# Third set's moments and second set's scaling by VectorE inside the second layer's attentions, with another order of stages there and in the last mixture

## The chip, the cores and the metric

The kernel runs on one core of one Trainium2 chip. The metric is the device time of one execution in microseconds (us). Six runs of the kernel before took 1302.55, 1298.72, 1302.09, 1302.53, 1300.03 and 1296.94 us; their median is 1301.06 us.

## The reference

The reference is a pre-LN decoder of two layers over `x`, 32 batches of 128 positions of 128 features, with a context `ctx_1024` of the same shape. Everything is float32. Cut to what matters:

```python
x = x + attn0(layernorm(x))              # 16 heads of 8, rotated, softmax
x = x + xattn0(layernorm(x), ctx)        # 16 heads of 64, relu between two output weights
x = x + moe0(layernorm(x))               # 16 experts, 4 per token, chosen by groups, and a shared one
x = x + attn1(layernorm(x))              # random features: exp(phi), no softmax
x = x + xattn1(layernorm(x), ctx)        # 16 heads of 8, softmax
h = layernorm(x)                         # (x - mean) / sqrt(var + 1e-5)
logits = h @ gate_w.T
sel = top_k(logits + expert_bias, 4)     # 4 of 16 experts for each token
w = softmax(logits[sel])
routed = sum(w[e] * (silu(h @ w1[e].T) * (h @ w3[e].T)) @ w2[e].T for e in sel)
x = x + routed + (silu(h @ sw1.T) * (h @ sw3.T)) @ sw2.T
```

## The kernel before

**Tiling.** The 32 batches are 8 groups `x[g]` of 4 batches (`GB = 4`), one SBUF tile `[128 positions, 4, 128 features]` for each; two groups, 8 batches, are a set, so there are four sets, 0 to 3. Layer 0's attentions and its mixture take the first 785 us. Layer 1's two attentions (`second_layers`, some 785 to 1053 us) go group by group, four steps a group; the last mixture (`last_layer`, some 1052 to 1297 us) follows.

**The last mixture.** Sets 0, 2 and 3 (`SETS = (0, 2, 3)`; `n2`, `n3` are the latter two) are sent by expert: each token's normalised row is written by GpSimd's indirect DMA to the rows of its four experts in DRAM (`way_out`, L2236, 32 transfers a set), four tiles of 128 rows, a quad, are loaded by SyncE with the weights of their experts (`rows_of`, L2299, tiles `rows` and `row_weights`), turned (`rows_turned`, L2317, `prows`), multiplied (`rows_up`, `pg<-hrows` and `sgrows`; `rows_down`), and written back on ScalarE's queue (`rows_out`). GpSimd gathers each token's four rows again (`way_back`, L2349, `back`, 32 a set), and VectorE adds them to `x` with the token's four weights (`added`, L2360). There are 33 quads, one a step, from step 3 on. Set 1 (groups 2 and 3) is computed densely: every expert over every token (`chunk_up`, `chunk_down`), its `sg` scaled by a broadcast of the token's weight, the `share`, that SyncE fetches in blocks of 1 MB (`fetched`, L2276).

Before a set can be sent it is normalised, its logits are made (`routing`), experts chosen (`chosen`, in `route`), and places counted (`placed`, L2163 to L2217; the list of each tile's expert, `of`, comes at its end; `owned` transposes it on TensorE, `powner`, and makes it readable for the address registers). Sets 0 and 2 go through this inside the second attentions: `rnorm`, `rscaled`, `rturn`, `routing`, `choose`, `send` are stages of the last mixture that `second_layers` writes between the attention's own, six groups in all (0 and 1, 2 and 3, 4 and 5). Set 3, groups 6 and 7, is ready only when the attentions end, and is normalised in the last mixture.

**Two ways to normalise.** `moments` (L1138, L1139) makes mean and variance of a group on VectorE, two instructions a batch. The inverse root is made by GpSimd's `pow` (`power`, L1120) in `norm_factors`, or on VectorE by three Newton steps (`rsqrt`, L1109 to L1114; with the addition of epsilon at L1172, 12 small instructions a group) in `norm_factors_by_vector`. `normed` (L1149) then scales the four batches; batches 1 and 3 are done by the engine `second`, GpSimd unless named otherwise:

```python
for b in range(GB):
    eng = second if b % 2 else nc.vector
    eng.tensor_scalar(n[:, b, :], x[g][:, b, :], mv[:, b, 0:1], r[:, b : b + 1], ALU.subtract, ALU.mult)
```

In the last mixture's stages inside the attentions it was `second=nc.gpsimd`; the scaled rows of sets 1 and 2 are kept in the context tiles (`ctx` in the profile), those of set 0 in a tile of weights no longer used (`wide`). Set 3's are the tiles `xr`, scaled by VectorE alone.

**Order.** `steps` takes a list of stages, each with its first step, its distance in steps and its count, and writes them step by step. In each step, the stages of the first list advance in turn by one piece, and after each of them one piece of the stages in `between` is written, the first in that list that still has one. A stage with a fifth entry may not begin before the stages named there are written. From step `as_written` on (8 in `second_layers`, 0 in `last_layer`) the engines take the instructions in the order in which they were written: TensorE, VectorE, ScalarE, GpSimd, and in the last mixture SyncE too. So the order of the two lists is the order of the instructions of one step on every engine's queue, and a wait at the head of a queue holds everything behind it.

**Tile names of the second attentions.** In the first of them `xn`, `pxn` are the normalised group and its transposition, `pS` and `sb` the sums over keys (`totals`), `fsums`, `frec` the products with the queries (`average`), `proj` the output weights (`finish`). In the second, `pk`, `k`, `pval`, `vs`, `pq`, `qb` are its projections, `scores`, `e`, `sums` the softmax, `by_token`, `rec`, `a`, `aT` the division and transposition, `proj` the output.

Of the kernel before, what the change touches and what calls it, by code (L numbers as in the profile page):

```python
# [17 lines left out]
GB = 4  # L18
GT = GB * S
NG = T // GT  # L20
# [939 lines left out]
def fast_decoder(ctx: ExitStack, tc: tile.TileContext, ins, spans, out: bass.AP):  # L960
# [3 lines left out]
    nc = tc.nc  # L964
# [13 lines left out]
    last = [None]  # L978
# [164 lines left out]
    def normed(wk, g, mv, r, n=None, second=nc.gpsimd):  # L1143

        if n is None:
            n = wk.tile([128, GB, D], F32, name="xn", bufs=2)
# [3 lines that stand above are left out]
            if b % 2:  # L1150
                yield
        return n
# [728 lines left out]
        yield  # L1881
        return comb

    def mixture(tag, W, route, per, last, weights_of, more={}, kept=lambda g: None):


        nch = E // per
# [6 lines left out]
            xn[g] = yield from norm_factors(g)  # L1894

        def scaled(wk, g):
            xn[g] = yield from normed(wk, g, *xn[g], kept(g))

        def turn(wk, g):
            pool, bufs = (edge, 2) if g in groups(0) else (wk, 5)  # L1900
# [188 lines left out]
    class Tables:  # L2089


        def __init__(self, spare, C):

            self.C = C
            self.xn, self.ones, self.masks, self.parts, self.places, self.of, self.owners, self.placing = ({} for _ in range(8))
# [152 lines left out]
    def last_layer(tag, W, stages, of_expert, tables):  # L2248
# [7 lines left out]
        factors, held, ys, sgs, outs = ({} for _ in range(5))  # L2256
        of_set = lambda n: range(n * NBR // GB, (n + 1) * NBR // GB)

        def norm(g):
            factors[g] = yield from norm_factors_by_vector(g)  # L2260

        def scaled(g):
            xn[g] = wk.tile([128, GB, D], F32, name="xr", bufs=2)
            yield from normed(wk, g, *factors.pop(g), xn[g], nc.vector)

        def turn(g):
            hs[g] = wk.tile([128, GT], F32, name="hx", bufs=2)
# [193 lines left out]
        to_send = lambda n, many: [(n, [(u, k) for u in range(i, i + many) for k in range(4)]) for i in range(0, NBR, many)]  # L2461
        once = lambda stage, k, s: (lambda _: stage(k), s, 1, 1)
        steps(
            fetch_at(4, 3),
            fetch_at(7, 18),
            (each(rows_turned, quads), Q, 1, NQ),
            fetch_at(5, 9),
            fetch_at(6, 9),
            fetch_at(0, 0),
            fetch_at(1, 0),  # L2470
            fetch_at(2, 0),
            (several(each(rows_of, quads), (0, 1)), 0, 1, 1),
            fetch_at(3, 0),
            (ups, 0, 1, LAST),
            (each(rows_down, quads), Q + 1, 1, NQ),
            once(routing, n3, 7),
            once(tables.owned, n3, 15),
            (each(rows_up, quads), Q, 1, NQ),
            (several(turn, of_set(n3)), 5, 1, 1),
            (downs, 0, 1, LAST),  # L2480
            (lambda _: not_ok(wk), 29, 1, 1),
            (lambda _: chunk_up(*last), 50, 1, 1),
            (last_parts, 52, 1, GB + 1),
            once(tables.owned, n2, 3),
            between=[
                (each(added, batches(n3)), 39, 2, NBR),
                once(tables.placed, n2, 1),
                once(chosen, n3, 8),
                once(tables.placed, n3, 9),
                (each(way_back, batches(n3)), 38, 2, NBR),  # L2490
                (each(rows_of, quads[2:]), Q, 1, NQ - 2),
                (each(tables.way_out, to_send(n3, 1)), 10, 1, NBR),
                (each(added, batches(n2)), 30, 1, NBR),
                once(several(norm, of_set(n3)), None, 3),
                (each(tables.way_out, to_send(n2, 2)), 1, 1, 4),
                once(several(scaled, of_set(n3)), None, 5),
                (each(way_back, batches(n2)), 29, 1, NBR),
                (each(way_back, batches(0)), 17, 1, NBR),
                (each(added, batches(0)), 21, 1, NBR),
            ],  # L2500
            as_written=0,
            others=("SP",),
# [190 lines left out]
    def second_layers(stages, early, late, after, tables):  # L2693

        wk = phase("l1", attention_psum)
        late.append(wk)
        norm, scaled, turn_in, project, turn, features_q, features_k, totals, average, finish = stages
        xnorm, xscaled, xvalues, xkey, xturn, xproject, xweights, xaverage, xfinish = l1_xattn(early, wk)
        rnorm, rscaled, rturn, routing, choose, send, *_ = after
        R = NBR // GB  # L2700
        first = lambda stage: lambda g: stage(early, g)
        later = lambda stage: lambda g: stage(g + 1)
        norm_, scaled_ = later(norm), later(scaled)
        of_four = lambda stage, b, at: (lambda g: stage(g * GB + b), at, 4, NG)
        to_send = [(u, k) for u in range(NBR) for k in range(4)]

        steps(
            (finish, 9, 4, NG),
            (features_q, 3, 4, NG),
            (lambda _: tables.owned(0), 35, 1, 1),  # L2710
            (totals, 5, 1, NU),
            (later(turn), 6, 4, NG - 1),
            (xvalues, 11, 4, NG),
            (lambda _: send(early, 1), 43, 1, 1),
            (features_k, 4, 4, NG),
            (later(project), 5, 4, NG - 1),
            of_four(xweights, 1, 13),
            of_four(xweights, 2, 14),
            (xturn, 11, 4, NG, xscaled),
            (average, 5, 1, NU),  # L2720
            (xfinish, 17, 4, NG),
            (first(rturn), 20, 4, 3 * R),
            of_four(xweights, 3, 15),
            (later(turn_in), 4, 4, NG - 1),
            (xaverage, 13, 1, NU),
            (first(routing), (24, 33, 42), 1, 3),
            of_four(xweights, 0, 12),
            (xproject, 11, 4, NG),
            (xkey, 10, 4, NG),
            between=[  # L2730
                (lambda _: choose(2, 6), 43, 1, 3),
                (lambda k: tables.place(0, (7, -1)[k]), 32, 1, 2),
                (first(rscaled), 19, 4, 3 * R, xturn),
                (xscaled, 11, 4, NG),
                (lambda _: choose(1, 3), 35, 1, 6),
                (scaled_, 2, 4, NG - 1),
                (lambda _: choose(0, 3), 27, 1, 6),
                (first(rnorm), 18, 4, 3 * R),
                (xnorm, 9, 4, NG),
                (norm_, 0, 4, NG - 1),  # L2740
                (lambda i: tables.way_out(0, to_send[3 * i : 3 * i + 3]), 36, 1, 11),
            ],
            as_written=8,
        )
# [49 lines left out]
    with tc.tile_pool(name="l1early", bufs=1, reuse_waits="tile") as early:  # L2794
        late = []
        W1A, W1X, L = (load(name, nc.sync, early) for name in ("w1a", "w1x", "later"))
        with scope():
            stages = []

            def l1_setup(_, k):  # L2800
                stages.extend(l1_attn(early, late))

            mixture_layer(
                "l0f",
                mixture0,
                (l1_setup, *(lambda _, k, i=i: stages[i](k) for i in range(5))),
            )
# [46 lines left out]
```

## Time and profile before

| | |
|---|---|
| median of six runs | 1301.06 us (1296.94 to 1302.55) |
| the profiled execution's own time | 1298.54 us |
| its span | 1296.8 us, granted clock 0.982 on average |
| TensorE matmuls (PE) | 1205.9 us busy, 93% |
| weight loads (PEld) | 802.8 us, 62%, beside PE |
| VectorE (DVE) | 855.7 us, 66% |
| ScalarE (ACT) | 589.3 us, 45% |
| GpSimd (POOL) | 533.4 us, 41% |

The shares are averages over stages with different limits. The stretch that the change touches, from 980 us on, looks like this (PE and VectorE busy in 20 us each, from the windows):

| window, us | PE | DVE | POOL | granted clock |
|---|---|---|---|---|
| 980 to 1000 | 16.29 | 17.08 | 2.58 | 0.92 |
| 1000 to 1020 | 18.15 | 17.67 | 8.75 | 1.00 |
| 1020 to 1040 | 13.50 | 10.36 | 16.69 | 0.83 |
| 1040 to 1060 | 17.43 | 16.14 | 15.64 | 1.00 |
| 1060 to 1080 | 17.40 | 17.50 | 12.85 | 1.00 |
| 1080 to 1100 | 18.76 | 10.62 | 15.36 | 1.00 |

A row of a timeline gives start, duration, engine, line, operation, tile out<-in, shapes, a count, and in brackets the idle time before the row and what ended it.

### The profile page before, as it was taken

The page shows a single profiled execution, that of the slowest core. Times are in us where ns is not written, and L with a number is a line of the kernel's source. Part 1 is how long each engine was busy: PE and PEld are TensorE (multiplying, and loading weights), DVE is VectorE, ACT ScalarE, POOL GpSimd, SP SyncE. Part 2 cuts the span into 40 slices and gives each one's busy share as a digit, 9 for nine tenths or more (in the row PEclk, how much of TensorE's full clock was granted, in tenths as well). Part 3 has the DMA queues.
Part 4 walks back from the last instruction along what each step waited for, and adds up shares of the span by engine and source line. Part 5 has one row for each costly group of instructions (what it writes and reads, how often), then busy time and mean ns, then how long its engine had stood idle before and what let it go on. Part 6 is the DMA issues. An engine that isn't in the chain of part 4 may idle for free. (4 is left out here: it accounts for less than half of the span.)

```text
span 1296.8 us, 27100 instructions
## 1 busy us (share of the span) xinstructions
PE 1205.9 (93%) x10588; PEld 802.8 (62%) x10588; DVE 855.7 (66%) x2298; ACT 589.3 (45%) x884; POOL 533.4 (41%) x715
## 2 busy tenths in 40 slices
PE   7779999999999999988999998899998789999997
PEld 5447667777777778753444444666666446787754
DVE  5746767686868667566866554688888776524563
ACT  4545444545455543432332224466664544554532
POOL 6244242434342213413200012456542677477775
PEclk9889999999999999999999999999999899999998
DMA  9401132111111111244541602000000049899933
GB/s 326 143 2 34 34 109 64 35 35 34 35 35 34 35 34 35 72 96 113 113 100 33 132 1 104 1 3 2 2 2 3 24 157 307 288 318 286 287 94 102
DMA packets 82895, 118.62 MB, mean 91 GB/s; under 512 B 9032, under 2 KB 58056, under 8 KB 81352
## 3 DMA queue, kind: packets, MB, share of 16 engines
q1 hardware_dynamic: 70280, 92.95, 25.7%
q0 software_dynamic: 6144, 12.60, 3.3%
q10 hardware_dynamic: 6336, 11.26, 2.3%
q8 instruction: 86, 1.41, 0.5%
q14 instruction: 49, 0.40, 0.1%
HBM read 89.71 MB, written 27.07 MB: 90 GB/s over the span
## 5 line engine op out<-in xcount | busy, mean ns | idle before, releaser
L1311 ACT ACTIVATE e<-scores 128x1024 f32<-128x1024 f32 x128 | 124.0, 1021 | 79.3 <-PE scores L981 79.3
L981 PE MATMUL y<-sg,wide 128*128 128x512 f32 (+1 forms) x206 | 107.1, 611 | 5.3 <-DVE sg L2374 4.7
L2349 POOL DMA_INDIRECT back<-rows_out,place x96 | 92.8, 967 | 31.4 <-issue 24.7
L1149 POOL TENSOR_SCALAR xn<-x,mv,r 128x128 f32<-128x128 f32 x78 | 69.3, 893 | 86.6 <-PE pxn L1158 80.0
L1565 ACT ACTIVATE e<-xscores 128x1024 f32<-128x1024 f32 x64 | 62.0, 1021 | 68.1 <-PE xscores L981 68.1
L1326 DVE STREAM_TRANSPOSE by_token<-sums 128x512 f32<-128x512 f32 x64 | 45.4, 710 | 70.2 <-PE sums L981 70.0
L1120 POOL TENSOR_SCALAR r<-mv 128x4 f32<-128x4 f32 x46 | 14.4, 315 | 183.3 <-DVE mv L1139 183.2
L1120 POOL TENSOR_SCALAR r2x<-mv 128x2 f32<-128x2 f32 x16 | 3.7, 234 | 204.4 <-DVE mv L1139 204.4
L1960 ACT ACTIVATE sg<-pg 128x512 f32<-128x512 f32 x63 | 37.6, 597 | 108.2 <-PE pg L981 100.4
L981 PE MATMUL scores<-qb,k 32*128 32x512 f32 x512 | 75.8, 663 | 10.8 <-ACT e L1311 6.7
L1961 DVE TENSOR_TENSOR sg<-sg,pu 128x512 f32<-128x512 f32 x63 | 43.2, 686 | 54.9 <-PE pu L981 54.7
L981 PE MATMUL sums<-e,v 128*32 128x128 f32 x2048 | 73.1, 285 | 0.7 <-ACT e L1311 0.7
L981 PEld LDWEIGHTS sums<-e,v 128*32 128x32 f32 x2048 | 55.5, 113 | 25.1 <-issue 11.4
L981 PE MATMUL po<-e,v 128*64 128x128 f32 x1024 | 65.1, 277 | 4.3 <-DVE v L1579 4.3
L1613 ACT COPY av<-po 128x512 f32<-128x512 f32 x64 | 37.5, 586 | 65.1 <-PE po L981 64.0
L981 PEld LDWEIGHTS y<-sg,wide 128*128 128x128 f32 x206 | 33.5, 189 | 53.3 <-DVE sg L1963 29.3
L981 PE MATMUL pval<-wide,ctx 128*128 128x512 f32 x128 | 63.2, 615 | 2.3 <-DVE by_token L1326 2.3
L981 PE MATMUL pqk<-h,wide 128*128 128x256 f32 x256 | 64.2, 396 | 0.7 <-ACT h L1161 0.7
L981 PEld LDWEIGHTS po<-e,v 128*64 128x64 f32 x1024 | 55.0, 137 | 13.0 <-DVE v L1579 4.4
L981 PE MATMUL pu<-hx,wide 128*128 128x512 f32 x116 | 60.2, 601 | 0.0
L1544 DVE COPY qk<-pqk 128x512 f32<-128x512 f32 x54 | 36.7, 685 | 35.2 <-PE pqk L981 35.1
L981 PE MATMUL pqk<-ctx,wide 128*128 128x256 f32 x256 | 59.5, 385 | 0.0
(361 smaller groups left out, 2960.1 us busy)
## 6 DMA issues: line engine op xcount, KB each, us to landing
row_weights<-in_w1f_dram SPq DMA_DIRECT2D x99, 192.0 KB
factor<-factors SPq DMA_DIRECT2D x64, 256.0 KB
share<-combined SPq DMA_DIRECT2D x28, 512.0 KB
rows_in<-in_few SPq DMA_DIRECT2D x33, 256.0 KB
rows<-rows_in SPq DMA_DIRECT2D x33, 256.0 KB
rows_out<-yrows ACTq DMA_DIRECT2D x33, 256.0 KB
share<-combined SPq DMA_DIRECT2D x8, 1024.0 KB
wide<-in_w1f_dram SPq DMA_DIRECT2D x1, 3272.0 KB
```

The costliest lines, as they stand in the source:

```text
L981: last[0] = nc.tensor.matmul(*args, **kw)
L1120: nc.gpsimd.tensor_scalar(t, src, add, None, ALU.add)
L1149: eng.tensor_scalar(n[:, b, :], x[g][:, b, :], mv[:, b, 0:1], r[:, b : b + 1], ALU.subtract, ALU.mult)
L1311: nc.scalar.activation(e[-1], ps[:, bass.ts(n, 2)].rearrange("p c i s -> p (c i) s"), AF.Exp, scale=scale)
L1326: nc.vector.transpose(tt.rearrange("p i t r -> p (i t r)"), po.rearrange("p i s -> p (i s)"))
L1544: nc.vector.tensor_copy(t, ps)
L1565: nc.scalar.activation(e[-1], ps[:, n].rearrange("p r c s -> p (r c) s"), AF.Exp, scale=scale)
L1613: nc.scalar.copy(avs[w][n][:, :, bass.ts(b, S)], po)
L1960: nc.scalar.activation(sg, pg, AF.Silu)
L1961: nc.vector.tensor_tensor(sg, sg, pu, ALU.mult)
L2349: nc.gpsimd.indirect_dma_start(out=outs[n, u][:, k], out_offset=None, in_=rows_out[n], in_offset=bass.IndirectOffsetOnAxis(ap=places[n][:, ...
```

## The change

The diff has three parts. (1) `mixture` takes a tuple `by_vector`; the groups in it are scaled by VectorE alone. The last mixture passes (4, 5), the second set's groups. (2) Set 3's moments and Newton steps leave step 3 of `last_layer` and become `last_norms` in steps 42 and 46 of `second_layers`, one group each; the factors are handed over in `tables.factors`. (3) The stages of both lists stand in another order, and some begin a step or two earlier or later: `send` 43 to 42; in the last mixture the fetches 3, 4, 5 and 7, `owned` of set 3 (15 to 16), its `turn` (5 to 6), its `way_out` (10 to 11), the gathers of the three sets (17 to 19, 29 to 28, 38 to 37), two of the additions (21 to 22, 30 to 31), and the last group's parts (50 to 52, 52 to 54). No stage's arithmetic changes.

```diff
-    def mixture(tag, W, route, per, last, weights_of, more={}, kept=lambda g: None):
+    def mixture(tag, W, route, per, last, weights_of, more={}, kept=lambda g: None, by_vector=()):
...
         def scaled(wk, g):
-            xn[g] = yield from normed(wk, g, *xn[g], kept(g))
+            second = nc.vector if g in by_vector else nc.gpsimd
+            xn[g] = yield from normed(wk, g, *xn[g], kept(g), second)
...
-        def norm(g):
-            factors[g] = yield from norm_factors_by_vector(g)
...
-            yield from normed(wk, g, *factors.pop(g), xn[g], nc.vector)
+            yield from normed(wk, g, *tables.factors.pop(g), xn[g], nc.vector)
...
         steps(                                   # last_layer
-            fetch_at(4, 3),
-            fetch_at(7, 18),
+            fetch_at(0, 0),
             (each(rows_turned, quads), Q, 1, NQ),
-            fetch_at(5, 9),
+            fetch_at(1, 0),
+            (several(each(rows_of, quads), (0, 1)), 0, 1, 1),
             fetch_at(6, 9),
-            fetch_at(0, 0),
-            fetch_at(1, 0),
+            fetch_at(5, 8),
+            fetch_at(4, 1),
             fetch_at(2, 0),
-            (several(each(rows_of, quads), (0, 1)), 0, 1, 1),
-            fetch_at(3, 0),
             (ups, 0, 1, LAST),
+            fetch_at(3, 1),
+            (last_parts, 54, 1, GB + 1),
             (each(rows_down, quads), Q + 1, 1, NQ),
+            once(tables.owned, n2, 3),
+            once(tables.owned, n3, 16),
+            (lambda _: chunk_up(*last), 52, 1, 1),
             once(routing, n3, 7),
-            once(tables.owned, n3, 15),
             (each(rows_up, quads), Q, 1, NQ),
-            (several(turn, of_set(n3)), 5, 1, 1),
+            (several(turn, of_set(n3)), 6, 1, 1),
             (downs, 0, 1, LAST),
             (lambda _: not_ok(wk), 29, 1, 1),
-            (lambda _: chunk_up(*last), 50, 1, 1),
-            (last_parts, 52, 1, GB + 1),
-            once(tables.owned, n2, 3),
+            fetch_at(7, 17),
             between=[
+                once(chosen, n3, 8),
+                once(tables.placed, n2, 1),
+                (each(way_back, batches(n3)), 37, 2, NBR),
+                (each(tables.way_out, to_send(n3, 1)), 11, 1, NBR),
+                (each(way_back, batches(0)), 19, 1, NBR),
+                (each(tables.way_out, to_send(n2, 2)), 1, 1, 4),
+                (each(added, batches(0)), 22, 1, NBR),
+                once(tables.placed, n3, 9),
+                (each(rows_of, quads[2:]), Q, 1, NQ - 2),
+                once(several(scaled, of_set(n3)), None, 5),
+                (each(way_back, batches(n2)), 28, 1, NBR),
+                (each(added, batches(n2)), 31, 1, NBR),
                 (each(added, batches(n3)), 39, 2, NBR),
-                once(tables.placed, n2, 1),
-                once(chosen, n3, 8),
-                once(tables.placed, n3, 9),
-                (each(way_back, batches(n3)), 38, 2, NBR),
-                (each(rows_of, quads[2:]), Q, 1, NQ - 2),
-                (each(tables.way_out, to_send(n3, 1)), 10, 1, NBR),
-                (each(added, batches(n2)), 30, 1, NBR),
-                once(several(norm, of_set(n3)), None, 3),
-                (each(tables.way_out, to_send(n2, 2)), 1, 1, 4),
-                once(several(scaled, of_set(n3)), None, 5),
-                (each(way_back, batches(n2)), 29, 1, NBR),
-                (each(way_back, batches(0)), 17, 1, NBR),
-                (each(added, batches(0)), 21, 1, NBR),
             ],
...
+        def last_norms(i):                       # second_layers
+            g = SETS[-1] * R + i
+            tables.factors[g] = yield from norm_factors_by_vector(g)
...
         steps(
-            (finish, 9, 4, NG),
             (features_q, 3, 4, NG),
             (lambda _: tables.owned(0), 35, 1, 1),
+            (finish, 9, 4, NG),
+            (xvalues, 11, 4, NG),
+            (lambda _: send(early, 1), 42, 1, 1),
             (totals, 5, 1, NU),
-            (later(turn), 6, 4, NG - 1),
-            (xvalues, 11, 4, NG),
-            (lambda _: send(early, 1), 43, 1, 1),
-            (features_k, 4, 4, NG),
+            (xturn, 11, 4, NG, xscaled),
             (later(project), 5, 4, NG - 1),
             of_four(xweights, 1, 13),
+            (later(turn), 6, 4, NG - 1),
             of_four(xweights, 2, 14),
-            (xturn, 11, 4, NG, xscaled),
+            (xfinish, 17, 4, NG),
+            (features_k, 4, 4, NG),
+            (first(rturn), 20, 4, 3 * R),
             (average, 5, 1, NU),
-            (xfinish, 17, 4, NG),
-            (first(rturn), 20, 4, 3 * R),
...
             between=[
                 (lambda _: choose(2, 6), 43, 1, 3),
-                (lambda k: tables.place(0, (7, -1)[k]), 32, 1, 2),
+                (scaled_, 2, 4, NG - 1),
                 (first(rscaled), 19, 4, 3 * R, xturn),
                 (xscaled, 11, 4, NG),
+                (lambda _: choose(0, 3), 27, 1, 6),
                 (lambda _: choose(1, 3), 35, 1, 6),
-                (scaled_, 2, 4, NG - 1),
-                (lambda _: choose(0, 3), 27, 1, 6),
+                (last_norms, (42, 46), 1, R),
+                (xnorm, 9, 4, NG),
                 (first(rnorm), 18, 4, 3 * R),
-                (xnorm, 9, 4, NG),
                 (norm_, 0, 4, NG - 1),
+                (lambda k: tables.place(0, (7, -1)[k]), 32, 1, 2),
                 (lambda i: tables.way_out(0, to_send[3 * i : 3 * i + 3]), 36, 1, 11),
             ],
...
-        mixture1 = mixture("l1f", W1F, route, 1, True, of_expert, {2: cx[0], 3: cx[1], 4: cx[4], 5: cx[5]}, tables.kept)
+        mixture1 = mixture("l1f", W1F, route, 1, True, of_expert, {2: cx[0], 3: cx[1], 4: cx[4], 5: cx[5]}, tables.kept, (4, 5))
```

More of the change, by code (lines that the diff above doesn't have):

```diff
@@ L2094, in __init__ @@
             self.C = C
-            self.xn, self.ones, self.masks, self.parts, self.places, self.of, self.owners, self.placing = ({} for _ in range(8))
+            self.xn, self.ones, self.masks, self.parts, self.places, self.of, self.owners, self.placing, self.factors = ({} for _ in range(9))
             self.one = by_rows.tile([128, 1], F32, name="one")
@@ L2255, in last_layer @@
         xn, places, parts, owners = tables.xn, tables.places, tables.parts, tables.owners
-        factors, held, ys, sgs, outs = ({} for _ in range(5))
+        held, ys, sgs, outs = ({} for _ in range(4))
         of_set = lambda n: range(n * NBR // GB, (n + 1) * NBR // GB)
-        def norm(g):
-            factors[g] = yield from norm_factors_by_vector(g)
         def scaled(g):
             xn[g] = wk.tile([128, GB, D], F32, name="xr", bufs=2)
-            yield from normed(wk, g, *factors.pop(g), xn[g], nc.vector)
+            yield from normed(wk, g, *tables.factors.pop(g), xn[g], nc.vector)
         def turn(g):
```

## The prediction

> **What bounds the kernel now.** I read the chain of waits from its end first, then GpSimd's timeline backwards to where it last stood still, then TensorE's timeline for the waits ahead of that point, then the windows for the clock. The chain ends in GpSimd's gathers (columns: start, us, what):
>
> ```profile
> 1286.36 0.94 POOL back L2349
> 1287.30 0.30 issue
> 1287.61 2.60 DMA back<-rows_out,place
> 1290.21 0.03 issue
> 1290.24 0.02 DVEq L2360
> 1290.26 0.04 issue
> 1290.30 0.36 DVE x L2360
> ```
>
> The next view is GpSimd's timeline; the bracket is the idle time before the row and what ended it:
>
> ```profile
> 1031.61 1.76 POOL L1149 TENSOR_SCALAR ctx<-x,mv,r 128x128 f32<-128x128 f32 x2
> ...
> 1123.42 0.96 POOL L2236 DMA_INDIRECT rows_in<-xr,place  x1 [13.88 <-DVE expert_ends L2214]
> ...
> 1247.93 0.94 POOL L2349 DMA_INDIRECT back<-rows_out,place  x1 [2.44 <-DVE x L2360]
> ```
>
> From 1123.42 to the last gather at 1287.61 GpSimd issues 32 scatters and 96 gathers, some 1.25 us apart, and stands still once, for 2.44 us. So the end is the start of the third set's scatters plus 165.1 us, 2.44 of them a wait. That wait is labelled DVE, but `added` of that time was long done; the transfer that frees these gathers is the last quad's `rows_out`, issued at 1244.64 behind TensorE. The change can act on the end in two ways only: the scatters' start, and those 2.44 us. TensorE's timeline shows what stands ahead of both:
>
> ```profile
> 1024.52 1.32 PE L1158 MATMUL pxn<-in_few,xn 128*128 128x128 f32 x4 [2.84 <-DVE xn L1149]
> ...
> 1032.53 0.44 PE L1158 MATMUL pxn<-in_few,ctx 128*128 128x128 f32 x2 [1.09 <-POOL ctx L1149]
> 1033.43 0.33 PE L1158 MATMUL pxn<-in_few,ctx 128*128 128x128 f32 x1 [0.45 <-POOL ctx L1149]
> ...
> 1051.32 0.49 PE L981 MATMUL proj<-in_w1x,aT 128*128 128x128 f32 x2 [0.91 <-DVE aT L1333]
> ...
> 1069.21 0.66 PE L2317 MATMUL prows<-in_few,rows 128*128 128x128 f32 x4 [1.64 <-DMA rows<-rows_in]
> ...
> 1072.99 0.71 PE L981 MATMUL pg<-hrows,row_weights 128*128 128x128 f32 x4 [0.96 <-DMA row_weights<-in_w1f_dram]
> ...
> 1083.36 1.12 PE L981 MATMUL y<-sg,wide 128*128 128x512 f32 x2 [1.24 <-DVE sg L2374]
> ...
> 1175.56 1.12 PE L981 MATMUL y<-sg,wide 128*128 128x512 f32 x2 [1.33 <-DVE sg L2374]
> ```
>
> Last, windows, with busy time of PE, PEld, DVE, ACT, POOL and then the granted clock:
>
> ```profile
> 996.00:1000.00 4.00, 3.33 (x49) 2.63 (x50) 3.56 (x13) 0.69 (x1) 1.27 (x2) 0.58 0.00 0
> 1024.00:1026.00 2.00, 1.48 (x8) 0.88 (x12) 1.16 (x5) 0.12 (x1) 1.78 (x3) 0.50 0.22 70
> 1040.00:1060.00 20.00, 17.43 (x198) 10.49 (x197) 16.14 (x51) 11.33 (x15) 15.64 (x18) 1.00 0.48 175
> 1060.00:1080.00 20.00, 17.40 (x64) 9.23 (x63) 17.50 (x63) 5.48 (x10) 12.85 (x14) 1.00 0.71 241
> ```
>
> VectorE is nearly full exactly where the moments are to go, and after a wait of 2.84 us TensorE ran at half clock.
>
> **The change part by part, against the profiled execution (span 1296.8, own time 1298.54 us).**
>
> *Orders up to 1020 us.* `totals` behind `xvalues`, `average` behind `xaverage` and the like exchange neighbours on TensorE; its work stays the same. In each group the second attention's last `xn` now follows one `vs` copy (0.28 us). One of the waits, at 971 us, grows by 0.35 to 0.5; the wait of 0.86 at 988 is covered by a projection that moves ahead of it, but VectorE is full from 981.7 to 996.2, so the `fsums` at 996.67 start no sooner. I take +0.5 (bounds −1 and +3: one wait of 0.86 gone; 0.4 in each of eight groups).
>
> *The second set's scaling.* Four GpSimd instructions go (1.76 for two). VectorE gets four at 0.26 to 0.35, beside transposes that keep it busy 10.36 of 20 us in this stretch. TensorE's waits of 1.09 and 0.45 go, but its next scores wait for ScalarE's `qb` to 1034.15 instead of starting at 1034.69: −0.5, not −1.54. It cancels the +0.5. GpSimd's first-set scatters run back to back from 1033.5, so they end 1.8 us earlier, near 1063.4; the first quad's rows and weights follow, and TensorE's 1.64 and 0.96 can go: −2.6. Nothing is queued behind the removed instructions that wants them later.
>
> *Moments of group 6, in step 42.* In today's place one batch costs 0.42 + 0.40 us per pair of moments with its overlap, and the Newton block 1075.31 to 1077.65, 2.34 us; the four batches add 1.6: 3.9 us a group. Their new place lies among the last head transposes (1.61 us a unit) between 1043 and 1051, where VectorE idles 1.1 us in all. Of 3.9 that slack takes 1.1, and overlaps 0.5 by my estimate; the last `aT` becomes ready 2.3 us later, and behind it stand the last projection, the mixture's first `pg`, the first share's issue, all of it: +2.3. Bounds: 0 (all of it slipped into gaps) and 3.9.
>
> TensorE then waits 0.9 + 2.3 less what it can still do, some 2.6 us, in one piece. At 1.69, 2.05 and 2.84 us waits the trace has half clock behind, at 2.12 and 1.64 not. Half clock costs 2.1 us in the row at 996 (sums 1.93 where others take 1.08) and 3.2 at 1024. I take full clock, since the stretch before it is dense, and keep 3.2 in the range.
>
> [...]
>
> *Moments of group 7, in step 46.* They lie between the second set's place operations, which stand at 1063 to 1068.7 on VectorE, and the first `sg`. Of their 3.9 us some 3.2 stand ahead of `of`, the set's list of owners, which is ready at about 1068.7 + 2.3 + 3.2 = 1074.2. `owned(n2)` is the new wait: its transposition, now ahead of the first quad's `pg<-hrows` and formerly behind it (1077.01), holds TensorE's queue, and with it `hrows`, `pu`, the next `y`. That quad's `pg`, today at 1071.43, would come at 1071.43 − 1.64 + 2.3 = 1072.1, so TensorE waits some 2.2 us there (2.1 by the difference): +2.2 (bounds 0 and 5.3, half of the 10.5 us over which both groups stand today). The second set's scatters start some 5 us later; behind them GpSimd waits 13.88 us for the third set anyway, so this costs nothing, as long as that wait exceeds 5.
>
> *What the last layer gets back.* VectorE loses the moments between 1071.27 and 1081.8, so the `sg` for 1083.36 is there: −1.24. The third set's mask is ready 0.25 sooner. Sum at the scatters: 0.5 − 0.5 − 2.6 + 2.3 + 2.2 − 1.24 − 0.25 = +0.4, say +0.5: they start near 1123.9. The share that now goes ahead of the second quad's rows is 1 MB, about 2.6 us at the 400 GB/s that windows of full transfers show; those rows then land near 1084.6 with TensorE there near 1085. I count nothing, and 2.6 as the upper bound.
>
> *`added` of the first set one step later.* Four `y<-sg` (idle before them 1.33, 0.53, 0.93 and 0.70, 3.49 us between 1174 and 1206) wait because VectorE stands in `added` for a gather's transfer. A step later the gathers have landed. I keep about 1 us of it, for places where they have not; TensorE reaches the last quad some 2.5 us sooner, and this with the later scatter start closes GpSimd's wait: −2.44 at most, and I take it all.
>
> Sum: +0.5 − 2.44 = −1.9 us, 1296.6 on the profiled execution's scale. The median of the runs stands at 1301.06, 2.5 above the profiled one, so the forecast is 1299.2. A measurement of this kernel can tell about 0.3%, 3.9 us.
>
> Against moving elementwise work to VectorE while GpSimd sends speaks one row: a scatter beside VectorE's `xr` scaling took 1.41 where its neighbours took 0.95 (1125.94); the scatters beside four more such scalings would lose at most 4 × 0.46 = 1.8, ahead of a wait.
>
> **The rivals.** *Faster: the new work slips in.* If VectorE's order lets the last `aT` pass and `of` comes before TensorE needs it, neither +2.3 nor +2.2 arises: the scatters start 2.6 + 1.24 + 0.25 = 4.1 sooner, and with 2.44 the end is 6.5 earlier: 1294.5. For it: 16.14 of 20 us busy leaves gaps. Against it: those gaps are elsewhere than between 1043 and 1051.
>
> *Slower: VectorE's moments are paid by TensorE, at half clock.* Place: the last projection near 1051 to 1054. The wait there passes 2.8 us, as the one at 1024 does, and the next 6 us run at half clock: +3.2 on top of +0.5; and the two groups cost their upper halves, 1.6 and 1.5 more: scatters +6.8, the end +6.8 − 2.44 = +4.4, 1305.5. It decides from a scatter start later than 1123.42 + 2.44 + 3.9 = 1129.8. For it: the 2.84 row, and a stretch without slack. Against it: the first-set rows come sooner, so part of any delay falls into the 2.6 us that TensorE waits there already.
>
> *The change does not do what it says* (scalings still bound by something else on GpSimd): out, for the order of its instructions is otherwise the same.
>
> **How the numbers follow.** Forecast 0.40, own range 1295.5 to 1303; faster rival 0.32, around 1294.5; slower rival 0.28, around 1305.5. Below 1297.2 (faster by 0.3%) lie a third of the forecast, 0.13, and nine tenths of the faster rival, 0.29: 0.42. Above 1305.0 lie 0.26 of the slower one and 0.02 of the forecast: 0.28. The rest, 0.30, is no difference to tell. The range 1291.5 to 1307 takes in both rivals' centres and the uncertain terms on either side, and leaves out a tenth at each end.
>
> **What would show it.** In the profile after: GpSimd's first scatters end near 1063; the last `aT` near 1053.6; a TensorE wait ahead of `powner`; no wait at the first `prows` nor ahead of the `y` at 1083; scatters of `xr` near 1123.9; no GpSimd wait near 1247. A clock of 0.5 after 1054 points to the slower rival; scatters before 1121 to the faster. A chain that does not end in GpSimd's gathers would make the whole sum wrong.

## The result and the profile after

The changed kernel takes 1304.81 us (median of 41 runs, 1295.22 to 1310.09); the kernel before takes 1301.41 us over 83 runs beside it. The ratio is 1.0028, with a 95% interval of 1.0018 to 1.0038: slower by some 3.6 us, where 1.9 us less was forecast. The profiled execution took 1305.84 us, its span 1304.1 us, its granted clock 0.974.

Its views are read in the order of before. GpSimd's timeline first:

```profile
1073.12 0.96 POOL L2237 DMA_INDIRECT rows_in<-ctx,place  x1 [7.58 <-DVE expert_ends L2215]
...
1132.27 0.96 POOL L2237 DMA_INDIRECT rows_in<-xr,place  x1 [18.30 <-DVE expert_ends L2215]
...
1294.73 0.94 POOL L2347 DMA_INDIRECT back<-rows_out,place  x1 [0.30 <-issue]
```

The wait of 2.44 us ahead of the last gathers is gone, as forecast: from the third set's first scatter to the last gather it is now 1294.73 - 1132.27 = 162.5 us, before 164.2 (the prediction's 165.1 counts to the end of that gather's instruction). But the scatters start later. TensorE's timeline shows why:

```profile
1032.55 1.14 PE L981 MATMUL scores<-qb,k 32*128 32x512 f32 x8 [1.43 <-ACT qb L2683]
1035.81 2.09 PE L981 MATMUL scores<-qb,k 32*128 32x512 f32 x8 [2.12 <-ACT e L1311]
...
1050.09 1.08 PE L981 MATMUL sums<-e,v 128*32 128x128 f32 x32 [2.09 <-DVE v L2130]
1053.00 0.49 PE L981 MATMUL proj<-in_w1x,aT 128*128 128x128 f32 x2 [1.19 <-DVE aT L1333]
1054.56 0.49 PE L981 MATMUL proj<-in_w1x,aT 128*128 128x128 f32 x2 [1.07 <-DVE aT L1333]
...
1072.35 0.60 PE L2315 MATMUL prows<-in_few,rows 128*128 128x128 f32 x4
...
1074.50 0.27 PE L2230 MATMUL powner<-in_few,of 128*1 128x128 f32 x1
...
1083.81 1.02 PE L981 MATMUL y<-sg,wide 128*128 128x512 f32 x2
1090.31 1.09 PE L2315 MATMUL prows<-in_few,rows 128*128 128x128 f32 x4 [5.47 <-DMA rows<-rows_in]
```

A row without a bracket waited for nothing worth showing: so with the first quad's `prows`, `powner` and the `y` at 1083.81. Then TensorE stands 5.47 us for the rows of the third quad. They are the rows that the prediction and the expectations call the second quad's, as quads are counted from 0; here they are quad 2's. The chain of waits runs through their transfer. The windows add the clock (the column after the five busy times):

```profile
1074.56 15.61 DMA rows<-rows_in
1090.17 0.14 issue
1090.31 1.09 PE prows L2315 x4
```

```profile
1085.00:1091.00 6.00, 0.69 (x4) 0.73 (x5) 0.28 (x2) 0.00 (x0) 4.57 (x5) 0.87 0.94 337
1090.00:1098.00 8.00, 7.70 (x32) 5.66 (x33) 2.93 (x8) 2.63 (x5) 5.90 (x7) 0.61 0.66 197
1098.00:1110.00 12.00, 11.29 (x71) 7.72 (x69) 4.14 (x6) 6.22 (x13) 9.26 (x10) 1.00 0.77 235
```

At a clock of 0.61 the eight us from 1090 on lose another 3.1 us (8 x 0.39). What the transfer waited for stands on SyncE's queue. In the kernel before (row weights left out):

```profile
1051.84 1.31 SPq L2276 DMA_DIRECT2D share<-combined  x3
1066.47 0.32 SPq L2299 DMA_DIRECT2D rows<-rows_in  x1
...
1072.65 0.90 SPq L2276 DMA_DIRECT2D share<-combined  x2
1073.60 0.43 SPq L2299 DMA_DIRECT2D rows<-rows_in  x1
```

and in the changed one:

```profile
1055.08 0.81 SPq L2274 DMA_DIRECT2D share<-combined  x2
1066.87 0.32 SPq L2297 DMA_DIRECT2D rows<-rows_in  x1
...
1073.18 1.32 SPq L2274 DMA_DIRECT2D share<-combined  x3
1074.56 0.69 SPq L2297 DMA_DIRECT2D rows<-rows_in  x1
```

Five blocks of shares, 1 MB each, go out ahead of quad 2's rows in both. Before, three of them went at 1052, into a queue with little in it (a DMA share of 0.21 in the 8 us ahead), and two stood right before the rows; now it is two and three. Those rows are issued into a full queue: the next view is the kernel before, with the DMA share as the last column but one.

```profile
1072.00:1090.00 18.00, 15.80 (x94) 11.44 (x94) 14.16 (x55) 5.95 (x12) 13.72 (x15) 1.00 1.00 366
```

**A scale for comparing profiles.** The program up to the second attentions is the same in all kernels, yet their first transposition (`prot`) starts anywhere from 781 to 788 us in the twelve profiles from chips on which before takes 1300 us. So the table counts from it. "Quad 2" is the start of that quad's `prows`, "scatters" the third set's first, in us after `prot`.

| kernel | prot | last proj | quad 2 | scatters | last gather | end |
|---|---|---|---|---|---|---|
| before | 787.99 | 263.3 | 296.4 | 335.4 | 499.6 | 508.8 |
| changed | 782.45 | 272.1 | 307.9 | 349.8 | 512.3 | 521.7 |

By these two profiles the changed part lost some 13 us, by the timed runs 3.6. A single profile doesn't size a change this small; it names places, and the timed ratios of the experiments weigh them.

### The profile page after: what moved, and what is told of

Same layout as the page of the kernel before. It is cut to its first block, busy times and chain, and to the rows that moved or that the text cites. A ratio compares the mean times of both kernels' runs of the same rounds, so it can differ in the third digit from the quotient of the medians.

```text
span 1304.1 us, 27103 instructions
## 1 busy us (share of the span) xinstructions
PE 1213.9 (93%) x10588; PEld 806.2 (62%) x10588; DVE 857.4 (66%) x2302; ACT 589.6 (45%) x884; POOL 530.9 (41%) x711
## 4 chain that ended last, share of the span: by engine, by line
PE 71%; DVE 11%; DMA 7%; POOL 4%; ACT 3%; issue 2%; SPq 1%; ACTq 0%; DVEq 0%; POOLq 0%
PE pu L981 8%; PE po L981 8%; PE pg L981 8%; PE pqk L981 7%; PE y L981 6%; PE pval L981 4%; PE xscores L981 4%; PE scores L981 4%; PE sums L981 3%; DMA factor<-factors 2%; DMA rows<-rows_in 2%; PE pyrows L981 2%; PE proj L981 2%; PE xsums L981 2%; PE pS L981 1%
## 5 line engine op out<-in xcount | busy, mean ns | idle before, releaser
L981 PE MATMUL po<-av,wide 128*128 128x256 f32 x256 | 59.6, 386 | 0.0
```

Of the source, the lines that this page charges most:

```text
L981: last[0] = nc.tensor.matmul(*args, **kw)
```

## The experiments

Theory Q says that the queue of transfers made it slower: quad 2's rows behind one more block of shares. Theory M blames the moments, put where VectorE is nearly full (busy 6.77 of the 8 us from 1044 to 1052 in the kernel before); theory O the new order inside the second attentions. A fourth part, the gathers' steps, should gain.

**First study: two slower chips.** Here the kernel before itself takes 1423 to 1427 us. In the eight profiles taken here, none of them of the kernel before, the other engines stand still for long stretches while GpSimd issues scatter after scatter, as in this row of the changed kernel:

```profile
1214.22 2.07 PE L981 MATMUL pyrows<-row_weights,sgrows 128*128 128x128 f32 x8 [29.05 <-DVE sgrows L2332]
```

VectorE and ScalarE start again there 5 us after the end of the third set's last scatter (1208.44). What holds them isn't in the profile, and stays open. Of these eight runs mainly the ratios to before on the same chip are used.

The changed kernel again:

> The changed kernel itself once more, beside the three that follow, for a second profile. In the first profile, measured from the first transposition of the second attentions, the third set's scatters start 14.4 us later than before (1132.27 - 781.95 against 1123.42 - 787.5), while the medians differ by only 3.4 us. Theory: part of the 14.4 is the clock, which halves after waits in some executions and not in others; then this profile again shows the wait for the second quad's rows (5.47 us) and the late last aT (+2.5 us), but not every half-clock stretch of the first. Rival: the 14.4 us repeat, and the early part of the program (5.5 us shorter in the first profile) is what differs between the two medians. Time: 1.0028 of before by either.

Measured: 1.0036 (1.0011 to 1.0061). The loss repeats on this chip. The wait ahead of quad 2 is 3.85 us, the last projection 278.0 us after `prot`.

One fetch put back:

```diff
             fetch_at(1, 0),
+            fetch_at(2, 0),
             (several(each(rows_of, quads), (0, 1)), 0, 1, 1),
...
-            fetch_at(2, 0),
```

> The changed kernel with one fetch moved back: the third block of shares (1 MB) is issued ahead of the first two quads' rows again, so that two blocks and not three stand between them and the second quad's rows. Theory Q (the queue of transfers is what made it slower): the wait of 5.47 us ahead of the second quad's transposition falls by 2.6 us or goes, with the half clock behind it; 3 to 6 us faster than the changed kernel, ratio to before 0.998 to 1.0005. Theory M (VectorE's moments): nothing changes beyond 1 us, ratio 1.002 to 1.003.

> The same kernel as in the first study (third block of shares ahead of the first two quads' rows). There TensorE, VectorE and ScalarE stood still for 23 to 29 us at a time behind GpSimd's transfers, before as after, and hid what is looked for; this is the run again. Theory Q: the wait ahead of the second quad's transposition falls from 5.5 to under 3 us, and the half clock behind it goes: 3 to 6 us faster than the changed kernel, ratio to before 0.998 to 1.0005. Theory M: ratio stays at 1.002 to 1.003.

Measured: 1.0034 (1.0012 to 1.0056) and 1.0079 (1.0050 to 1.0107). The wait fell from 3.85 to 2.19 and 1.72 us, and no time came of it: against theory Q, on these chips. Why it doesn't pay here is open.

The moments put back into step 3 of the last mixture (`last_norms` out of the second attentions, `once(several(norm, of_set(n3)), None, 3)` back in):

> The changed kernel with the third set's moments and Newton steps back in step 3 of the last mixture. Theory M (the moments in the second attentions delay the last aT by 2.5 us, and the sums behind VectorE's v by 1.6 us): the last projection comes 2.5 to 4 us sooner, the list of owners 3 us sooner, ratio to before 0.9995 to 1.0005. Theory Q: TensorE only comes sooner to rows that land when they land, so the wait ahead of the second quad's transposition grows by what is gained, and the ratio stays at 1.002 to 1.003.

> The third set's moments back in the last mixture, once more. Theory M: the last projection 2.5 to 4 us sooner and all that follows with it, ratio 0.9995 to 1.0005. Theory Q: the wait ahead of the second quad's transposition grows by what is gained, ratio 1.002 to 1.003.

Measured: 1.0052 (1.0021 to 1.0082) and 1.0037 (0.9999 to 1.0074): not faster than the changed kernel. Nothing for theory M. The sooner last projection did not come (280.0 and 280.8 us after `prot`, with the moments moved 278.0), and the wait ahead of quad 2 did not grow, as theory Q had it, but was 0.34 and 1.80 us.

The list of the second attentions as before, with `last_norms` in it:

> The changed kernel with the list of stages of the second attentions in the order of before; the moments stand in it ahead of rnorm, in steps 42 and 46, and the second set's scaling stays with VectorE. Theory Q: no change against the changed kernel, ratio 1.002 to 1.003, with the wait ahead of the second quad's transposition there. Theory O (the order in the second attentions costs 2 to 5 us up to 1015 us: a wait of 3.2 us ahead of fsums instead of 0.86 and 2.05, and a later first set of scores): 2 to 4 us faster, ratio 0.999 to 1.001.

Measured: 1.0052 (1.0023 to 1.0081). Nothing for theory O either.

The list and steps of the last mixture as before:

> The changed kernel with the list of stages of the last mixture, and its steps, as before; the moments stay in the second attentions and the second set's scaling stays with VectorE. Theory Q: no wait of 5 us ahead of the second quad's transposition, the waits for added come back (3.5 us, hidden behind GpSimd), ratio 0.998 to 1.000. Theory M, or a cause in the order of the second attentions: ratio 1.002 or above, with the last aT as late as in the changed kernel.

> The changed kernel with the last mixture's list and steps as before, once more. Theory Q: no wait of 5 us ahead of the second quad's transposition, ratio 0.998 to 1.000. Theories M and O: ratio 1.002 or above.

Measured: 1.0009 (0.9984 to 1.0034) and 1.0014 (0.9982 to 1.0047), the lowest ratios of the five. The intervals overlap, so this only points to the last mixture's list.

**Second study: chips on which before takes 1300 us.** This and the two studies behind it ran on three such chips; each ratio is to before on the same chip. The kernel before again, the moves alone, and two parts of the last mixture's list put back one by one:

> The kernel before itself, for its profile on the chip of the experiments. Every theory: the same stretches of 20 to 30 us in which the other engines stand behind GpSimd's transfers, the last projection some 270 us after the first transposition of the second attentions against 278 to 282 in the five kernels with the moments moved; 1420 to 1430 us.

Measured: 1299.84 us, with no such stretch: the guess that they would repeat is refuted, they belong to the other two chips. Last projection at 266.1, scatters at 338.0, end at 511.9 us after `prot`, so two profiles of one kernel differ by 3 us on this scale.

> The kernel before with the two moves alone: the third set's moments in steps 42 and 46 of the second attentions, the second set's scaling by VectorE; both lists of stages and all steps as before. Theory L (the last mixture's order and steps cost, the moves do not): ratio to before 0.998 to 1.001. Theory M (the moves cost, as VectorE is full there): 1.002 to 1.004.

Measured: 1300.17 us, ratio 1.0002 (0.9984 to 1.0019). The moments and the scaling cost nothing at the end that these runs can tell. They do delay the last projection (268.4 us after `prot`), with a wait of 3.44 us for VectorE's `v` (2.09 in the changed kernel), but the scatters start at 338.4.

The fetches put back (all eight, at the places and steps of before):

```diff
-            fetch_at(0, 0),
+            fetch_at(4, 3),
+            fetch_at(7, 18),
             (each(rows_turned, quads), Q, 1, NQ),
-            fetch_at(1, 0),
+            fetch_at(5, 9),
+            fetch_at(6, 9),
+            fetch_at(0, 0),
+            fetch_at(1, 0),
+            fetch_at(2, 0),
             (several(each(rows_of, quads), (0, 1)), 0, 1, 1),
-            fetch_at(6, 9),
-            fetch_at(5, 8),
-            fetch_at(4, 1),
-            fetch_at(2, 0),
+            fetch_at(3, 0),
...
-            fetch_at(3, 1),
...
-            fetch_at(7, 17),
```

> The changed kernel with all eight fetches of shares at the places and steps of before; every other stage of the last mixture's list in its new place. Theory Q (the queue of transfers ahead of the second quad's rows): back to 0.999 to 1.0015. Theory G (the gathers and additions, at other steps): stays at 1.003 to 1.006.

Measured: 1301.06 us, 1.0011 (0.9992 to 1.0031). No wait ahead of quad 2 is left (299.4 us after `prot`), and the scatters start at 338.5 instead of 349.8.

The gathers and additions put back to their steps of before (17, 29, 38; 21, 30):

> The changed kernel with the five stages of gathers and additions at their steps of before (17, 29, 38 and 21, 30), in their new places in the list. Theory G: back to 0.999 to 1.0015, with another pattern of GpSimd's stream of gathers. Theory Q: stays at 1.003 to 1.006.

Measured: 1309.79 us, 1.0065 (1.0038 to 1.0092). It is slower than the changed kernel, so these steps are a gain and not the cause. The wait that they had closed is back, in the same place as with the moves alone; first that kernel's row, then this one's:

```profile
1248.07 0.96 POOL L2347 DMA_INDIRECT back<-rows_out,place  x1 [2.63 <-DVE x L2358]
```

```profile
1259.74 0.95 POOL L2347 DMA_INDIRECT back<-rows_out,place  x1 [2.64 <-DVE x L2358]
```

**Third study: is one part enough?** The kernel before with the new fetches alone:

> The kernel before with one thing of the change: the eight fetches of shares at their new places and steps. Theory Q: enough by itself. The second quad's rows wait behind three blocks of shares, TensorE stands 5 us ahead of that quad's transposition and runs at half clock behind it; the third set's scatters start 5 to 8 us later, the end 3 to 6 us later: ratio 1.002 to 1.005. Rival: the queue hurts only together with the later attentions and the late list of owners; then 0.999 to 1.001 and a wait below 2 us.

Measured: 1305.44 us, 1.0033 (1.0016 to 1.0050): the whole loss, with neither the moves nor another order elsewhere. The row and the clock behind it:

```profile
1089.26 1.12 PE L2317 MATMUL prows<-in_few,rows 128*128 128x128 f32 x4 [4.46 <-DMA rows<-rows_in]
```

```profile
1085.00:1090.00 5.00, 0.74 (x4) 0.74 (x5) 0.00 (x0) 0.00 (x0) 3.83 (x4) 0.51 1.03 384
1090.00:1098.00 8.00, 8.00 (x39) 5.93 (x38) 3.53 (x9) 2.97 (x6) 6.03 (x7) 0.67 0.75 200
```

The kernel before with the gathers' and additions' new steps alone:

> The kernel before with one thing of the change: gathers and additions at their new steps (19, 28, 37 and 22, 31). GpSimd's wait of 2.4 to 2.6 us ahead of its last 32 gathers, there in the kernel before, with the moves alone and with the gathers put back, goes; nothing else changes. Expected 2 to 3 us faster, ratio 0.9975 to 0.9990, and the last gather 162.5 us behind the third set's first scatter instead of 164.2 to 165. Rival: the gathers then meet more transfers and each takes longer; ratio 0.999 to 1.001.

Measured: 1297.69 us, 0.9983 (0.9965 to 1.0001). GpSimd has no wait between its scatters and its last gather, which is 162.9 us after the first scatter. The size is as expected, 2.3 us; the interval just reaches 1.

Both moves and the gathers' steps, in the lists of before:

> Both moves and the gathers' new steps, with both lists and the fetches as before: the parts of the change that cost nothing or gain. The moves alone measured 1.0002. Expected 2 to 3 us below that, ratio 0.997 to 0.9995, no GpSimd wait ahead of the last gathers, no wait of 5 us for the second quad's rows.

Measured: 1300.53 us, 0.9992 (0.9975 to 1.0009): the 2 to 3 us expected did not show, though the interval takes them in. GpSimd has no wait ahead of the last gathers; a wait of 2.07 us ahead of quad 2 is left, with no half clock behind it.

> The changed kernel once more beside these three. Theory Q with the gathers' gain: 1.002 to 1.004, a wait of 4 to 6 us ahead of the second quad's transposition with half clock behind it, no GpSimd wait ahead of the last gathers.

Measured: 1304.66 us, 1.0028 (1.0010 to 1.0047), as in the first result. The wait ahead of quad 2 is 3.56 us this time, less than the 4 to 6 expected, with half clock behind it (0.79 on average from 1092 to 1100), and the scatters start at 346.8.

**Fourth study: how many blocks ahead of the rows.** The changed kernel with the one fetch put back, now on a chip where before takes 1301 us:

> The changed kernel with the third block of shares ahead of the first two quads' rows again, on a chip where before takes 1300 us. Theory Q: one block of 1 MB in its old place is most of it. The wait ahead of the second quad's transposition falls from 3.6 to 5.5 us to 2 us or less, TensorE's clock stays up behind it, ratio to before 0.999 to 1.0015, against 1.0028 for the changed kernel. Rival: all the fetches' places together make it, and this one alone leaves a wait above 3 us and 1.002 or more.

Measured: 1298.96 us, 0.9990 (0.9968 to 1.0012). The wait falls to 1.19 us and the clock stays up:

```profile
1083.01 0.63 PE L2315 MATMUL prows<-in_few,rows 128*128 128x128 f32 x4 [1.19 <-DMA rows<-rows_in]
```

```profile
1085.00:1090.00 5.00, 5.00 (x33) 3.83 (x32) 3.51 (x9) 1.95 (x4) 3.78 (x5) 1.00 0.96 310
```

One line of the list, with all else of the change in place, takes the loss away. From the chains, the time from issue to landing of quad 2's rows, behind two blocks in share2_first_c and moves_gathers and then behind three in after_third (15.61 in the first profile of the changed kernel):

```profile
1072.18 10.70 DMA rows<-rows_in
```

```profile
1075.19 11.27 DMA rows<-rows_in
```

```profile
1078.83 13.70 DMA rows<-rows_in
```

Both moves, the gathers' steps, and blocks 3 and 4 fetched behind quad 2's rows:

```diff
-            fetch_at(4, 3),
+            fetch_at(4, 6),
...
-            fetch_at(3, 0),
+            fetch_at(3, 4),
```

> Both moves and the gathers' new steps in the order of before, and the fourth and fifth blocks of shares fetched later, behind the second quad's rows (steps 4 and 6 for 0 and 3), so that nothing stands ahead of these rows in the queue. Theory Q turned round: the wait of 2.07 us ahead of the second quad's transposition goes, the third set's scatters start 1 to 2 us sooner, ratio 0.997 to 0.999, below both kernels. Rival: the shares then come late for the dense group and VectorE waits for them; 1.000 to 1.002.

Measured: 1297.11 us, 0.9979 (0.9962 to 0.9996), below both kernels. No wait is left ahead of quad 2 (296.0 us after `prot`), and VectorE waits for none of the shares fetched later; it waits 1.89 us for the very first, at 1060, as it does in the kernel before (1.35).

The landmarks of the runs of the second to fourth study, in us after `prot`:

| kernel | last proj | quad 2 | scatters | last gather | ratio |
|---|---|---|---|---|---|
| before, again | 266.1 | 298.7 | 338.0 | 503.0 | 1 |
| moves_only | 268.4 | 299.4 | 338.4 | 504.1 | 1.0002 |
| before_gathers | 265.1 | 297.6 | 336.6 | 499.5 | 0.9983 |
| moves_gathers | 265.6 | 298.3 | 338.8 | 499.4 | 0.9992 |
| moves_gathers_late | 266.1 | 296.0 | 335.5 | 497.8 | 0.9979 |
| fetches_back | 269.3 | 299.4 | 338.5 | 501.2 | 1.0011 |
| share2_first_c | 269.1 | 300.6 | 339.7 | 501.9 | 0.9990 |
| before_fetches | 264.7 | 301.5 | 343.6 | 509.0 | 1.0033 |
| after_third | 272.2 | 306.0 | 346.8 | 509.1 | 1.0028 |
| gathers_back | 272.2 | 307.5 | 348.1 | 513.2 | 1.0065 |

Every kernel with three blocks right ahead of the rows (the last three) starts its scatters 343.6 us or later, every other one 339.7 or earlier. On average the last gathers of the two groups stand 9.4 us apart, the times 6.3 (ratios of 1.0042 and 0.9994). Part of the larger figure arose ahead of any fetch: the `fsums` of about 1009 us stand 226.6 us after `prot` in after_third and gathers_back and 223.6 to 223.7 in share2_first_c and fetches_back, whose programs are the same up to there. Counted from these `fsums`, the scatters of the three start after 120.2 to 122.7 us and those of the others after 114.1 to 117.5, so the groups stay apart, by 5 us on average.

## Why the prediction failed, step by step

**The step that failed** is the sentence on the share: "I count nothing, and 2.6 as the upper bound." Moving the fetch was seen, and the 1 MB was priced at a row of full transfers, but as if it met only the rows. It went into a queue that was already full, with a DMA share of 1.00 over 1072 to 1090 in the kernel before. There one more block cost 2.4 to 4.9 us of landing (13.7 and 15.6 behind three blocks, 10.7 and 11.3 behind two), so 2.6 was no upper bound, and it came on top of a landing that had no slack (forecast 1084.6 against a need at 1085). TensorE, ready at 1084.8, stood 5.47 us, and the half clock cost 3.1 more. The forecast looked for half clock at the last projection, and not behind this wait. By itself this part, forecast at 0, measures +4.3 us (0.33% of 1300), half of the 5.47 + 3.1 that the first profile shows.

**Right in kind and size.** The wait ahead of the last gathers: forecast -2.44, gone in every kernel with the new steps, measured -2.3 by itself. The wait of 1.24 us at the `y` of 1083 went. Group 6's moments: the last projection follows the `plogits` of the last attentions by 9.07 us (1054.56 - 1045.49) instead of 6.58 (1051.32 - 1044.74), +2.5 where +2.3 was forecast. They stand in the chain as one block:

```profile
1046.32 0.19 DVE parts L1138
...
1049.59 0.16 DVE rv L1114
1049.75 0.19 DVE v L1098
```

**Right by luck.** The waits of 1.64 and 0.96 us at the first quad went too, but not because its rows came sooner. Behind the removed scalings the prediction saw nothing in GpSimd's queue that could wait. There was: the range check of the last group's reciprocals, which VectorE now delivers at 1053.8 instead of 1050.6.

```profile
1053.99 0.46 POOL L1345 TENSOR_SCALAR in_range<-rec 128x64 f32<-128x64 f32 x1 [2.82 <-DVE rec L1328]
```

So the first set's scatters end at 1065.5, and not near 1063.4 (before 1065.2; the `fsums` of 1009 us stand within 0.1 us of each other in the two profiles). The waits went because TensorE itself came later: it reached the first quad at 1072.35, where the terms give 1069.21 - 1.64 + 2.3 = 1069.9. The term of -2.6 was no gain.

**Wrong in size, without weight at the end.** The wait for `powner`, forecast at 2.2, didn't come: the list of owners was ready at 1073.4, not 1074.2, and TensorE, for the same lateness, reached it only at 1074.50. The second attentions' new order, forecast at +0.5 with +3 as its bound, delays the `fsums` of about 1009 us by 2.7 to 5.7 us: they stand 220.9 us after `prot` in before and 223.6 to 226.6 in the five profiles with the new order from chips of 1300 us (219.6 to 222.2 in those with the old one). Putting the old order back gained nothing (1.0052 on a slower chip), and the changed kernel with one fetch back, new order and all, is at 0.9990. Most of such a delay is gone by the scatters: fetches_back is 3.1 us behind before at the last projection and 0.5 at the scatters.

**The scaling.** The waits for GpSimd went and the scores wait 1.43 us for `qb`, as forecast. Whether the 0.5 us came can't be told, as the clock moves this stretch by more. Behind the next wait, 2.12 us as before, eight scores run at half clock, 2.09 us instead of 1.14, in all eight profiles with the move from chips of 1300 us. In the four without it they take 1.14; but in three of these the eight scores ahead of that wait, behind GpSimd's two waits, take 2.09 us instead, and only the profile that the prediction read has neither. From the `fsums` of 1009 to the last attentions' `plogits` it is 35.9 us in that one, 37.2 to 38.9 in the three, and 35.3 to 37.0 with the move (36.5 in the changed kernel).

**The rivals.** The slower one came nearest in time (1305.5), and its half clock at the last projection did come: the `pu` behind it takes 1.91 us instead of 1.02 in all five profiles with the new order from chips of 1300 us, where the forecast had taken full clock by estimate; with its neighbours that is 1.8 us (0.46 + 0.89 + 0.44). But share2_first_c has it too and is not slower than before, and moves_only, with the moments moved and half clock on that projection itself (1.65 us for six matmuls that take 0.94 in before), is at 1.0002. So that rival's half clock is there and not the cause, and that its figure came near is luck. The tested parts add up to +0.33 - 0.17 + 0.02 = 0.18%, against 0.28% measured; the rest, 1.3 us, lies within the intervals.

## What to carry to other kernels

Order by hand has to be priced on the transfer queues too: a prefetch that moves past a load with a near due time costs what the full queue makes of its bytes, here 2.4 to 4.9 us of landing for 1 MB at a DMA share of 0.99 to 1.00 (from 1075 to 1090 in the changed kernel, from 1072 to 1090 in the one before); the same bytes cost nothing that the runs can tell (0.9990) in a stretch where the queue had room (a share of 0.21 in the 8 us ahead, in the kernel before). When a change moves many things a little, first look for the one landing that had no slack; and size an effect of a few us by repeated times, as the first pair of profiles here differed by some 13 us where the timed runs differ by 3.6.

## What the hardware showed unexpectedly

The length of a single gap doesn't settle the clock here. In the stretch around 1030 us the kernel before (two profiles) and two kernels that differ from it only later have nearly the same waits: 1.1 to 1.3, 0.45 and 2.12 us. In the first profile the scores behind the 0.45 run at full clock; in the three others (here before_again) at half, and those behind the 2.12 at full in all four:

```profile
1034.69 1.14 PE L981 MATMUL scores<-qb,k 32*128 32x512 f32 x8
1037.95 1.14 PE L981 MATMUL scores<-qb,k 32*128 32x512 f32 x8 [2.12 <-ACT e L1311]
```

```profile
1033.17 2.09 PE L981 MATMUL scores<-qb,k 32*128 32x512 f32 x8
1037.38 1.14 PE L981 MATMUL scores<-qb,k 32*128 32x512 f32 x8 [2.12 <-ACT e L1311]
```

With the scaling moved, a wait of 1.43 us ends 1.1 us before the 2.12 begins, 3.55 us of rest in 4.7, and the scores behind it ran at half clock in eight of eight (2.09 us instead of 1.14). The kernel before has half clock behind shorter single waits too: behind 1.69 us at 822 (a clock of 0.57 from 822 to 826) and behind 2.05 us at 996 (0.58 from 996 to 1000), while behind 2.12 us at 1038 it is 1.00 (from 1035 to 1043). What decides between them, the runs here don't show.

On two chips TensorE stood for long stretches beside GpSimd's streams of indirect transfers (29.05 us in the row of the first study), and the kernel before took 1427 and 1423 us instead of 1300; the change measured 1.0036 on one of them and 1.0028 on the others.
